# Eight places for weighted samples instead of five, and the residual's tiles in memory that is given back, in a four-layer convolution kernel

## The chip, the cores and the metric

The kernel runs on one core of a Trainium2 chip. A core has a matrix engine (TensorE, in the profile PE, its weight loads PEld), VectorE (DVE), ScalarE (ACT), GpSimd (POOL) and SyncE (SP), which here only issues DMAs. Each engine works through its own queue in order; they wait for each other through semaphores. The metric is the device time of one execution in microseconds; the time before is the median of three runs.

## The reference

Four layers follow each other on `x` of shape (2, 256, 64, 64), in float32:

```python
x = _L0_conv_ref(x, ...)   # group norm, 4-head attention over 4096 pixels, projection; xn + proj
x = _L1_conv_ref(x, ...)   # adds a position term
x = _L2_conv_ref(x, ...)   # 1x1 to 64 channels, deformable 3x3 with a mask, 1x1 back, + x, relu
x = _L3_conv_ref(x, ...)   # two deformable 3x3 convolutions with 256 channels, + x
```

The last layer is the one that the change touches. It is `h = relu(group_norm(x)); h = deform_conv(h, 1); h = relu(group_norm(h)); h = deform_conv(h, 2); return h + x`, and a deformable convolution is

```python
off = conv1x1(depthwise7x7(h)) + b          # 9 taps x (y, x) for every pixel
samp[k] = bilinear(h, base + tap[k] + off)  # four corners, weighted, for every tap k
out = einsum('bckhw,ock->bohw', samp, w)    # sum over 256 channels and 9 taps
```

So every output pixel takes 9 samples of 256 channels, each the weighted sum of four pixels at an address that the data decide.

## The kernel before

**Four layers in one program.** `attention` holds layers 0 and 1, and drips parts of layer 2 into its own steps; `deform` holds layer 3 and, beside its first steps, the second image of layer 2. The order of the instructions on TensorE, ScalarE, VectorE and GpSimd is the order in which the Python code writes them. The order of the DMAs on SP is left to a scheduler, which may put a load where its tile first has memory.

**The loop of `deform`.** Layer 3 is four passes `n`: (image 0, convolution 1), (image 1, convolution 1), (image 0, convolution 2), (image 1, convolution 2). A pass has 8 blocks (`i`) of 512 pixels, a block 9 taps (`k`), a tap 4 groups (`j`) of 128 pixels. One group of one tap is a step, so a block has 36 steps, a pass 288 and the loop 1152. A step handles 128 pixels on the 128 partitions, with all 256 channels in a row. What one turn `s` of the loop writes, in this order:

- `gather(s + 8)`: GpSimd fetches for 128 pixels the four corners, 4 x 256 values each, into one of 10 places of `four` (L848). The first 72 steps load samples that were gathered earlier, through SP (L1448).
- `left(s + 3)` and `right(s + 2)`, only for "paired" steps: ScalarE scales the left two corners (L1471), VectorE adds the right two times their share (L1477), in place. In the first pass the steps from the third block on are paired, in the other passes every second one.
- `first(s + 1)`: takes a place for `smp`, the weighted sample, and ScalarE writes the first corner times its weight into it (L1486).
- `others(s)`: VectorE adds what is left into `smp`: one instruction for a paired step (L1490), three for another (L1496).
- `evacuate`, in every fourth turn: ScalarE copies the four transposed samples of a tap from PSUM into `st` (L1517).
- `product`: TensorE multiplies a transposed sample with the weights of its tap and sums in the bank `out` of the block (L1527), two half outputs `ob` of 128 channels, one bank each.
- `turn(s - 3)`: TensorE transposes the two halves of `smp` of step s - 3 into PSUM (L1508). With this the place of that `smp` is free.
- `due`: work put off to this turn. For convolution 1 ScalarE empties a finished bank (L1552), for convolution 2 VectorE does, adding the bias and the residual (L1563); SP stores the result (L1564).
- then the side work: steps of `seconds` (the second image of layer 2, whose code is `Bottleneck.conv`), of `image` (the normalized image that the next pass samples: L1372 on ScalarE, L1382 on TensorE, L1388 on VectorE) and of `offsets` (the addresses of the next pass: L805, L825 and L839 on TensorE, L816 and L834 on ScalarE, L738 to L778 on VectorE).

**Places.** A pool with `bufs=n` gives its tiles n places in turn. A tile that takes a place waits for the last reader of the tile that had it. `smp` (pool `df_s`, L1312) has 5 places of 1 KB per partition, so the write of `smp` s + 1 waits for the transposition of s - 4. The pool `work` (L1310) has two places of each name: among them `res` (L1559), the residual of a half block, 2 KB per partition, loaded by SP at L1560 when the bank is finished, and `imgt`.

**Memory given back.** The second image of layer 2 has pools of its own in an `ExitStack` called `inner` (L1584): gathers `bfour`, sums, transposed tiles and blocks `bx`. When its last step has run, `inner.close()` (L1622) gives their memory back, and the step after that may open pools there: `image` for pass 1 opens one for `x1`, the image that L1333 loads.

Of the kernel before, what the change touches and what calls it, by code (L numbers as in the profile page):

```python
# [11 lines left out]
F32 = mybir.dt.float32  # L12
# [8 lines left out]
P = 128  # L21
# [43 lines left out]
class Net:  # L65
# [1235 lines left out]
    def deform(self, bott):  # L1301
# [4 lines left out]
        tc, nc, a = self.tc, self.nc, self.a  # L1306
        with ExitStack() as ctx:
            gp = ctx.enter_context(tc.tile_pool(name="df_g", bufs=10))
            wp = ctx.enter_context(tc.tile_pool(name="df_w", bufs=1))
            work = ctx.enter_context(tc.tile_pool(name="df_work", bufs=2))  # L1310
            cp = ctx.enter_context(tc.tile_pool(name="df_c", bufs=4))
            sp = ctx.enter_context(tc.tile_pool(name="df_s", bufs=5))  # L1312
            tp = ctx.enter_context(tc.tile_pool(name="df_t", bufs=2))
            pmisc = ctx.enter_context(tc.tile_pool(name="df_pm", bufs=1, space=PSUM))
            pdw = ctx.enter_context(tc.tile_pool(name="df_pd", bufs=1, space=PSUM))
# [11 lines left out]
            def load(b, src, pool):  # L1327
                x[b] = pool.tile([P, 2, HW], F32, name=f"x{b}")
                src = src.rearrange("(cb p) n -> p cb n", p=P)
                for i in range(4):  # L1330
                    cols = slice(1024 * i, 1024 * i + 1024)
                    queue = (nc.gpsimd, nc.sync)[b]
                    queue.dma_start(x[b][:, :, cols], src[:, :, cols])  # L1333
# [26 lines left out]
            def image(b, l):  # L1360

                if l == 0:
                    load(b, self.x2d[b], ctx.enter_context(tc.tile_pool(name="df_x1", bufs=1)))
                sc, sh = yield from self.norm_steps(
                    stats[b], bott.gmask, V_GN_G[l], V_GN_B[l], ps
                )
                yield
                v = self.img3[b].rearrange("(y x) (s c) -> y x s c", x=GW, c=C)
                for i in range(NB):
                    for cb in range(2):  # L1370
                        xs = x[b][:, cb, 512 * i : 512 * i + 512]
                        nc.scalar.activation(  # L1372
                            xs, xs, AF.Relu, scale=sc[:, cb : cb + 1], bias=sh[:, cb : cb + 1]
                        )
                        yield
                    t = work.tile([P, 4, C], F32, name="imgt")
                    for g in range(2):
                        pt = ps([P, 2, C])
                        for j in range(2):
                            px = (4 * i + g * 2 + j) * P  # L1380
                            for cb in range(2):
                                nc.tensor.transpose(  # L1382
                                    pt[:, j, cb * P : cb * P + P],
                                    x[b][:, cb, px : px + P],
                                    self.ident,
                                )
                        yield
                        nc.vector.tensor_copy(t[:, g * 2 : g * 2 + 2, :], pt)  # L1388
                        if g == 1:
                            for r in range(2):  # L1390
                                for s in range(2):
                                    y0 = 8 * i + r + 1 - s
                                    dst = v[y0 : y0 + 7 : 2, 1 : W + 1, s, :]
                                    nc.sync.dma_start(
                                        dst.rearrange("j x c -> x j c"),
                                        t[64 * r : 64 * r + 64, :, :],
                                    )
                        yield
# [39 lines left out]
            def gather(s):  # L1438
                if s < ALL:
                    n, i, k, j = parts(s)  # L1440
                    b, l = layers[n]
                    fours[s] = gp.tile([P, 4, C], F32, name="four")
                    four = fours[s].rearrange("p s c -> p (s c)")
                    if n == 0 and i < EARLY:

                        queue = nc.gpsimd if s < AHEAD else nc.sync
                        m = 4 * k + j
                        queue.dma_start(four, self.samp_d[i][m * P : m * P + P, :])  # L1448
                        return
                    idx = corners[b, l, i][0]  # L1450
                    self.gather(four, self.img3[b], idx[:, j, k : k + 1])
# [15 lines left out]
            def left(s):  # L1467

                if paired(s):
                    uv = fours[s][:, 0:2].rearrange("p s c -> p (s c)")  # L1470
                    nc.scalar.mul(uv, uv, share(s, 0, 1))  # L1471

            def right(s):
                if paired(s):
                    four = fours[s].rearrange("p s c -> p (s c)")
                    uv = four[:, : 2 * C]
                    nc.vector.scalar_tensor_tensor(  # L1477
                        uv, four[:, 2 * C :], share(s, 1, 1), uv, ALU.mult, ALU.add
                    )

            def first(s):

                if s < ALL:
                    smps[s] = sp.tile([P, C], F32, name="smp")
                    scale = share(s, 0, 0) if paired(s) else weight(s, 0)
                    nc.scalar.mul(smps[s], fours[s][:, 0], scale)  # L1486
# [27 lines left out]
            def evacuate(u):  # L1514
                if 0 <= 4 * u < ALL:
                    sts[u] = tp.tile([P, 2, 512], F32, name="st")
                    nc.scalar.copy(sts[u], pts.pop(u))  # L1517
# [23 lines left out]
            def finish(n, i, ob, s):  # L1541

                b, l = layers[n]
                out = outs[ob]
                cols = slice(512 * i, 512 * i + 512)
                rows = slice(ob * P, ob * P + P)
                bias = self.vec[:, V_CB[l] + ob : V_CB[l] + ob + 1]
                if l == 0:
                    xs = x[b][:, ob, cols]

                    def first_layer():
                        nc.scalar.activation(xs, out, AF.Identity, bias=bias)  # L1552

                    due.setdefault(s + 1, []).append(first_layer)
                    due.setdefault(s + 3, []).append(
                        lambda: nc.vector.bn_stats(stats[b][:, ob, i, :], xs)
                    )
                else:
                    res = work.tile([P, 512], F32, name="res")  # L1559
                    nc.sync.dma_start(res, self.x2d[b][rows, cols])  # L1560

                    def second_layer():
                        nc.vector.scalar_tensor_tensor(res, out, bias, res, ALU.add, ALU.add)  # L1563
                        nc.sync.dma_start(self.out[b, rows, cols], res)  # L1564

                    due.setdefault(s + 2, []).append(second_layer)
# [14 lines left out]
                            self.steps = None  # L1581

            OFFS = 24
            inner = ExitStack()  # L1584
            second = bott.conv(1, bott.pools(inner, 8, 7), ps)
            for s in range(AHEAD):
                gather(s)
# [13 lines left out]
            for s in range(ALL + 16):  # L1601
                n = s // LAYER
                if s == LAYER:
                    stats[1] = self.norm_stats()
                gather(s + AHEAD)
                left(s + 3)
                right(s + 2)
                first(s + 1)
                others(s)
                if (s - 7) % 4 == 0:  # L1610
                    evacuate((s - 7) // 4)
                product(*divmod(s - 9, 4), s)
                turn(s - 3)
                for f in due.pop(s, ()):
                    f()
                last.follow(s)
                if seconds:
                    seconds.follow(s)
                    if not seconds.steps:
                        seconds = None  # L1620
                        stats[1] = bott.stats[1]
                        inner.close()  # L1622
                        images.append(Side(s, 0.9, image(*layers[1])))
                if s % LAYER == LAYER // 2 and 1 <= n < len(layers) - 1:
                    images.append(
                        Side(s, IMAGE / (LAYER // 2 - LEAD - 12), image(*layers[n + 1]))
                    )
                if s % LAYER == LAYER - LEAD - 8 and n + 1 < len(layers):
                    for o in images + offs:
                        for _ in o.steps or ():  # L1630
                            pass
                    images, offs = [], []
                    offs.append(Side(s, OFFS / BLOCK, offsets(*layers[n + 1])))
                for o in images + offs:
                    o.follow(s)
# [101 lines left out]
```

## Time and profile before

| | |
|---|---|
| median of 3 runs | 5122.12 us (5121.92 to 5128.18) |
| profiled execution | 5119.31 us |
| its span, first to last instruction | 5117.5 us |
| mean granted TensorE clock | 0.972 of full speed |
| busy: PE, DVE, ACT, POOL | 94%, 79%, 64%, 45% of the span |
| `deform` loop | 2990 us to the end |
| ACT writes of `smp` (L1486) | 1152, about 0.5 us each |
| transpositions (L1508) | 2304, 0.27 us each as modelled |

How to read it: the profile is one execution, its times are counted from the start of the span. A line of a wait list names the instruction that waited, then what released it. Matmul ends are modelled, and matmuls overlap, so a busy TensorE is not TensorE at its peak, and two transpositions that follow each other start closer together than one takes. "issue" as a releaser means that the engine waited for nothing that the profile shows. A name as L1486 is a line of the kernel before.

### The profile page before, as it was taken

Reading aid. Unit: us, or ns where it says so; the run is one execution under the profiler, and the core shown is the slowest. Engines: PE = TensorE matmul, PEld = TensorE weight load, DVE = VectorE, ACT = ScalarE, POOL = GpSimd, SP = SyncE. Lnnn points to the kernel's source line nnn. Section 1 sums busy time; section 2 is a strip of 40 time slices with the busy share of each in tenths; the row PEclk is TensorE's granted clock in tenths of the full one; section 3 lists DMA queues with packets and bytes.
Section 4 is the critical chain, followed back from the end, with each engine's and each line's share of the span. In section 5 each row is a group of like instructions: output and inputs, shape, how many; then the busy total and the mean of one; then the engine's idle time right before and its main releaser. Section 6 shows DMA issues by size and latency. Waiting matters only on the chain. (4 is left out here: it accounts for less than half of the span.)

```text
span 5117.5 us, 100364 instructions
## 1 busy us (share of the span) xinstructions
PE 4793.9 (94%) x38200; PEld 2669.1 (52%) x38200; DVE 4025.2 (79%) x7281; ACT 3251.1 (64%) x5869; POOL 2325.6 (45%) x2256
## 2 busy tenths in 40 slices
PE   8999999999999999999999956678999999999998
PEld 5555565555565555565555523334444444444444
DVE  6878867878768888677767668867788888888888
ACT  5676656666666666666656622247876766666666
POOL 0111111111106777565123257775777666666665
PEclk9999999999999999999999977779999999999999
DMA  5231121111112333332547767679999999999998
GB/s 173 61 97 53 43 69 49 35 47 31 55 53 80 103 98 105 93 86 70 164 147 284 274 223 236 202 237 349 358 339 352 363 376 358 366 396 344 349 352 331
DMA packets 367025, 997.68 MB, mean 195 GB/s; under 512 B 61372, under 2 KB 98810, under 8 KB 366542
## 3 DMA queue, kind: packets, MB, share of 16 engines
q0 software_dynamic: 196560, 690.41, 37.4%
q1 hardware_dynamic: 169438, 300.73, 18.0%
q8 instruction: 300, 4.92, 0.4%
q14 instruction: 183, 1.50, 0.1%
q10 hardware_dynamic: 544, 0.13, 0.0%
HBM read 855.36 MB, written 127.35 MB: 192 GB/s over the span
## 5 line engine op out<-in xcount | busy, mean ns | idle before, releaser
L598 ACT ACTIVATE e<-sc,low 128x1024 f32<-128x1024 f32 x1024 | 1146.2, 1119 | 742.3 <-DVE low L592 738.0
L848 POOL DMA_INDIRECT four<-img,didx x1080 | 1152.6, 1067 | 549.9 <-issue 140.3
L592 DVE TENSOR_REDUCE low<-sc 128x1 f32<-128x1024 f32 x1024 | 1205.0, 1218 | 231.7 <-PE sc L580 227.3
L1527 PE MATMUL out<-st,wc 128*128 128x512 f32 x2304 | 1224.8, 614 | 85.7 <-ACT st L1517 41.5
L580 PE MATMUL sc<-k,qs 64*128 64x512 f32 x2048 | 999.1, 606 | 0.5 <-DVE k L368 0.3
L639 PE MATMUL av<-et,v 128*64 128x256 f32 x8192 | 997.7, 386 | 0.0
L580 PE MATMUL sc<-k,q 64*128 64x512 f32 x2048 | 978.2, 605 | 0.0
L519 POOL TENSOR_TENSOR o<-o,f 128x1024 f32<-128x1024 f32 x63 | 149.5, 2373 | 1765.2 <-DMA f<-share_d 1007.7
L610 PEld LDWEIGHTS tt<-ident,e 64*128 64x128 f32 x16384 | 655.3, 139 | 512.9 <-issue 272.7
L629 ACT COPY et<-tt 128x512 f32<-128x512 f32 x1152 | 658.4, 584 | 171.8 <-PE tt L610 170.8
L610 PE MATMUL tt<-ident,e 64*128 64x64 f32 x16384 | 728.0, 227 | 36.3 <-ACT et L629 17.7
L627 DVE COPY et<-tt 128x512 f32<-128x512 f32 x896 | 612.5, 684 | 161.5 <-PE tt L610 160.9
L1496 DVE SCALAR_TENSOR_TENSOR smp<-four,dw,smp 128x256 f32<-128x256 f32 x1296 | 627.2, 484 | 140.5 <-ACT smp L1486 109.0
L639 PEld LDWEIGHTS av<-et,v 128*64 128x64 f32 x8192 | 554.0, 137 | 300.9 <-issue 48.4
L848 POOL DMA_INDIRECT bfour<-img,bidx x576 | 584.1, 1014 | 183.9 <-issue 94.8
L1508 PEld LDWEIGHTS pt<-ident,smp 128*128 128x128 f32 x2304 | 330.5, 144 | 633.9 <-issue 470.9
L1471 ACT ACTIVATE four<-four,dwt 128x512 f32<-128x512 f32 x648 | 465.0, 718 | 200.1 <-DMA four<-img,didx 196.6
L1477 DVE SCALAR_TENSOR_TENSOR four<-four,dwt 128x512 f32<-128x512 f32 x648 | 484.9, 748 | 112.6 <-ACT four L1471 110.2
L1527 PEld LDWEIGHTS out<-st,wc 128*128 128x128 f32 x2304 | 390.9, 196 | 339.3 <-issue 222.8
L580 PEld LDWEIGHTS sc<-k,qs 64*128 64x128 f32 x2048 | 346.9, 189 | 208.7 <-issue 116.8
L1508 PE MATMUL pt<-ident,smp 128*128 128x128 f32 x2304 | 448.8, 278 | 4.6 <-DVE smp L1496 3.1
L805 PE MATMUL pd<-x,wf 128*126 128x512 f32 x840 | 436.0, 601 | 0.0
(189 smaller groups left out, 4743.1 us busy)
## 6 DMA issues: line engine op xcount, KB each, us to landing
f<-share_d SPq DMA_DIRECT2D x128, 256.0 KB
four<-samp_d SPq DMA_DIRECT2D x64, 512.0 KB
xb<-xn SPq DMA_DIRECT2D x55, 512.0 KB
img<-imgt SPq DMA_DIRECT2D x96, 256.0 KB
four<-img,didx POOLq DMA_INDIRECT x1080
xa<-res SPq DMA_DIRECT2D x32, 512.0 KB
samp_d<-xb SPq DMA_DIRECT2D x32, 512.0 KB
xb<-in_x SPq DMA_DIRECT2D x20, 512.0 KB
```

What stands on the lines that cost most here:

```text
L580: nc.tensor.matmul(s[:, j, :], lhsT=q[u, i // 2][int(h != j)][halves[j], at : at + P], rhs=k[u][c][halves[j], h, :], start=True, stop=True,)
L592: nc.vector.tensor_reduce(low, s, AX.X, ALU.max, negate=True)
L598: nc.scalar.activation(e.rearrange("p j n -> p (j n)"), s, AF.Exp, bias=blk.low[:, g, c : c + 1], accum_out=blk.sum[:, g, c : c + 1],)
L610: nc.tensor.transpose(pt[:, m, :], e[half, m // 4, m % 4 * P : m % 4 * P + P], self.ident[half, half],)
L627: nc.vector.tensor_copy(dst, pt)
L629: nc.scalar.copy(dst, pt)
L639: nc.tensor.matmul(now["av"][halves[h], :], lhsT=v[u][c][:, m, halves[h]], rhs=ets[j][:, m, h, :], start=(m == 0), stop=(m == 7),)
L848: self.nc.gpsimd.indirect_dma_start(out=dst, out_offset=None, in_=img, in_offset=bass.IndirectOffsetOnAxis(ap=idx, axis=0),)
L1477: nc.vector.scalar_tensor_tensor(uv, four[:, 2 * C :], share(s, 1, 1), uv, ALU.mult, ALU.add)
L1496: nc.vector.scalar_tensor_tensor(smps[s], four[:, c], weight(s, c), smps[s], ALU.mult, ALU.add)
L1508: nc.tensor.transpose(pts[u][:, c, j * P : (j + 1) * P], smp[:, c * P : c * P + P], self.ident,)
L1527: nc.tensor.matmul(outs[ob], lhsT=wc[k][:, c, ob * P : ob * P + P], rhs=sts[u][:, c, :], start=(k == 0 and c == 0), stop=(k == K2 - 1 and ...
```

## The change

Three edits in `deform`. The pool of `smp` gets eight places of 1 KB instead of five, 3 KB per partition more. The two places of `res`, 4 KB per partition, leave the pool `work` and get a pool of their own, `df_r`, which is opened right after `inner.close()`, so in memory that the second image of layer 2 gave back. What is computed stays the same, and so do the instructions of the five engines.

```diff
@@ deform
-            sp = ctx.enter_context(tc.tile_pool(name="df_s", bufs=5))
+            sp = ctx.enter_context(tc.tile_pool(name="df_s", bufs=8))
@@ deform, finish
-                    res = work.tile([P, 512], F32, name="res")
+                    res = places["res"].tile([P, 512], F32, name="res")
                     nc.sync.dma_start(res, self.x2d[b][rows, cols])
@@ deform
-            inner = ExitStack()
+            inner, places = ExitStack(), {}
             second = bott.conv(1, bott.pools(inner, 8, 7), ps)
@@ deform, in the loop
                         inner.close()
+                        places["res"] = ctx.enter_context(tc.tile_pool(name="df_r", bufs=2))
                         images.append(Side(s, 0.9, image(*layers[1])))
```

## The prediction

> **What bounds the kernel now.** I read the busy times first, then a table of the deform part by stretches, then the waits of ScalarE and TensorE there, then one stretch in order of time.
>
> ```profile
> PE 4793.9 (94%) x38200; PEld 2669.1 (52%) x38200; DVE 4025.2 (79%) x7281; ACT 3251.1 (64%) x5869; POOL 2325.6 (45%) x2256
> ```
>
> TensorE is busy 94% of the span. The change touches only the deform loop, which starts at 2990 us (the first transposition of `smp`). Busy times there, by stretch (time, PE, PEld, DVE, ACT, POOL, granted clock, DMA share, GB/s):
>
> ```profile
> 2990.00:3513.00 523.00, 346.16 (x1090) 163.15 (x1089) 414.75 (x946) 183.83 (x322) 383.81 (x371) 0.77 0.73 240
> 3513.00:3979.00 466.00, 451.92 (x1658) 224.12 (x1657) 381.07 (x814) 363.17 (x636) 327.37 (x295) 0.99 0.96 357
> 3979.00:4275.00 296.00, 286.60 (x1066) 143.67 (x1065) 262.20 (x582) 207.86 (x363) 198.20 (x187) 0.99 0.98 367
> 4275.00:4560.00 285.00, 277.46 (x1033) 139.19 (x1032) 253.45 (x566) 197.31 (x341) 189.23 (x179) 1.00 0.99 372
> 4560.00:4603.00 43.00, 42.43 (x149) 21.68 (x148) 37.85 (x86) 29.07 (x51) 28.76 (x28) 1.00 1.02 396
> 4603.00:5002.00 399.00, 377.58 (x1355) 185.29 (x1354) 339.28 (x747) 262.18 (x454) 260.19 (x251) 1.00 0.96 350
> 5002.00:5117.00 115.00, 95.51 (x345) 46.54 (x343) 96.74 (x205) 74.72 (x131) 67.61 (x65) 1.00 0.86 328
> ```
>
> Up to 3513 GpSimd sets the pace: 371 instructions, busy 383.8 us, with about 0.30 us between two gathers (the releaser "issue", 0.3 us at most in the first 330 us) make 383.8 + 371 x 0.30 = 495 of 523 us. From 3513 to 5002 TensorE does: 95 to 99% busy at a granted clock of 0.99 to 1.00. So ScalarE's waits count only so far as they reach TensorE. ScalarE's two largest waits from 3513 on (total, times, longest):
>
> ```profile
> ACT smp L1486 <- PE pt L1508: 282.0, 330, 2.6
> ACT four L1471 <- DMA four<-img,didx: 115.6, 116, 3.8
> ```
>
> The 282.0 us are what the change aims at: a write of a new `smp` that waits for the transposition of an old one. Beside them, what TensorE itself waited for in the same stretch:
>
> ```profile
> PE out L1527 <- ACT st L1517: 18.0, 19, 3.1
> PE out L1527 <- DVE res L1563: 16.7, 16, 2.1
> PE out L1527 <- DVE floor L756: 14.0, 8, 1.8
> PE pm L1382 <- ACT x L1372: 11.5, 7, 4.7
> PE pm L1382 <- DVE imgt L1388: 5.3, 5, 2.0
> ```
>
> With four small groups (1.7, 1.0, 0.4, 0.2) that is 68.8 us: the most that a quicker ScalarE or VectorE can return from 3513 on. The "floor" group is the bank of a finished block too: L756 follows L1563 in VectorE's order.
>
> **The change part by part.** No instruction is added, removed or reordered on TensorE, VectorE, ScalarE or GpSimd; only waits differ, and two DMAs move on SP.
>
> *Eight places.* Before, L1486 at step s writes `smp` s+1 over that of s-4, transposed in step s-1. After, it is that of s-7, transposed in step s-4: three steps of slack more. But every fourth step ScalarE's L1517 copies four finished transpositions out, and waits for the last, made in the step before: the very bound that five places set. The lead is given back at each L1517; three steps in four run free. What that is worth shows near the end of a block (start, duration, instruction, idle before):
>
> ```profile
> 4607.66 0.51 ACT L1486 ACTIVATE smp<-four,dw 128x256 f32<-128x256 f32 x1 [1.81 <-PE pt L1508]
> ...
> 4608.20 1.52 DVE L1496 SCALAR_TENSOR_TENSOR smp<-four,dw,smp 128x256 f32<-128x256 f32 x3 [1.51 <-ACT smp L1486]
> ...
> 4610.23 0.99 ACT L1517 COPY st<-pt 128x1024 f32<-128x1024 f32 x1
> ...
> 4617.98 0.75 DVE L1563 SCALAR_TENSOR_TENSOR res<-out,vec,res 128x512 f32<-128x512 f32 x1
> ...
> 4618.87 1.10 PE L1527 MATMUL out<-st,wc 128*128 128x512 f32 x2 [1.72 <-DVE floor L756]
> ```
>
> From 4608.2 VectorE runs without a gap until TensorE has waited twice (1.72 us here, 1.31 us at 4622.58). With eight places the first line starts 1.81 us earlier and the second 1.51. But L1517 must still wait for the transposition that starts at 4609.40 and takes 0.38: it moves from 4610.23 to 4609.8, and the L1471 behind it from 4611.13 to 4610.75. VectorE's next L1477 (4612.28) reads what that leaves 0.7 us later, so starts at 4611.55. Its lead has shrunk from 1.5 to 0.72 us; from there it is continuous, L1563 and the product come 0.72 earlier, and the second wait keeps its length. So 0.72 us a block, of 3.03 waited. By stretch:
>
> - 4603 to 5002: seven such blocks, 7 x 0.72 = 5.0 of 21.4 us waited (bounds 0 and 21.4; the worked block decides).
> - 4275 to 4603: L1563 six times, 3.4 us. At 4328.83 ScalarE waits 2.65 us and again only L1517's 0.43 stays: 6 x 0.43 = 2.6. The waits for L1372 and L1388 (4.6) have a write held 0.83 us ahead of an L1372 that comes 1.21 late; half, 2.3. Together 4.9 (0 to 8.0).
> - 3979 to 4275: 9.4 us waited: L1388 and L1372 5.0, half is 2.5; L1496, L1517 and L834 4.0 in eight waits, a 0.2 each is 1.5. Together 4.0 (0 to 9.4).
> - 3513 to 3979: 14.0 us, of which 4.7 is L1372 behind the load of `x1` and stays; 6.5 is L1517, late because L1471 waits 34.6 us for gathers, which no place for `smp` brings sooner. I take 2.0 (0 to 9.3).
> - 5002 to 5117: 16.1 us; ScalarE waits 20.6 us for gathers, only 6.7 for transpositions. One block as above and a little: 1.0 (0 to 16.1).
> - 2990 to 3513: ScalarE waits 24.7 + 1.1 us for transpositions up to 3500, GpSimd's issue covers it: 0 (0 to 25.8).
>
> Sum: 16.9 us.
>
> *Waits that change engine.* In the built program ScalarE loses 598 semaphore instructions (L1486 869 fewer, L1517 274 more), and VectorE gains 432, nearly all before L1490, which now names the transposition that its ScalarE write no longer implies. They ask for a `smp` eight steps back, long transposed, so nothing queues behind them. Such an instruction on VectorE's queue (least, median, most ns):
>
> ```profile
> L1496 DVEq EVENT_SEMAPHORE  x506: 21/21/50, 2986.3 to 5102.9; - x169
> ```
>
> L1490 to L1496, with one between, start 0.39 us apart at 4610.31 (0.48 long); L1477 to L1490, with none, 0.67 (0.75 long): the overlap is 0.08 either way. I take 0; the bounds are 0 and 432 x 0.021 = 9.1 us, or 21.6 at the longest.
>
> *The residual's tiles.* The first two loads of L1560, at 2971.44, go behind the last L1078 of the second layer (3484.09) and ahead of its last store L1169 (3501.70) on SP. Issue is 0.82 us for both; 512 KB at 357 GB/s are 1.5 us, and 17 us are free: 0. Were they late, that store, the load of `x1` and the L1372 that already waits 6.2 us would slip by up to 1.5. At 2971 SP next issues at 2981.87, so what they leave gains nothing, 1.5 at most. Their first use is at 4276. GpSimd's queue is not passed.
>
> **Sum.** The profiled execution took 5119.3 us (span 5117.5), the median of the runs is 5122.1, 2.8 more. 5119.3 - 16.9 = 5102.4, and with 2.8 more 5105.
>
> **The rivals.** A measurement of this kernel can tell about 0.2% (10.2 us) from no change: 5111.9 to 5132.4.
>
> *Transfers hold it.* From 3513 to 4603 the DMA share is 0.96 to 1.02, and ScalarE waits 115.6 us for gathers in all. If they can come no faster, only the last two stretches gain: 6.0 us, 5116. Against it: 396 GB/s from 4560 to 4603, where others ran at 357 to 372. The Trainium skill, DMA: Bandwidth & Descriptors, Specifications, gives about 358 GB/s of HBM per core; by it the stretches at 357 to 372 have nothing left and 5116 is the time. The trace differs: it shows 396.
>
> *All bubbles go.* If the lead adds up over steps, TensorE's waits without the 4.7 for `x1` vanish: 64.1 us, 5058. For it: VectorE still idles 109.0 us for L1486 after 3513. Against it: L1517 every fourth step. The Trainium skill, Perfetto Trace Analysis, Identifying Performance Opportunities, says that the same gap repeating can mean too few buffers; by it this would be the case. The trace agrees on the repeating gap, and puts L1563 and L1517 at its end, not `smp`.
>
> *Slower: VectorE pays for the moved waits.* It is 85% busy from 4603 to 5002 and unbroken where TensorE waits. At 50 ns each and no gain, 432 cost 21.6 us: 5144. It decides from 24 ns each on (10.2 / 432) if nothing is gained, from 63 ns with 16.9 gained. Against it: the equal overlap above.
>
> **How the numbers follow.** Forecast (10 to 30 us gained) 0.52; transfers hold it, or the lead is given back entirely, 0.27; all bubbles (30 to 64) 0.11; slower 0.10. Faster 0.52 + 0.11 = 0.63, same 0.27, slower 0.10. The range runs from 5086, which leaves out most of the bubbles' case, to 5124, which leaves out the slower one; the forecast alone is 5092 to 5112.
>
> **What would show it.** L1486 waiting for L1508 falls from 282 to under 80 us, and L1517, which waited 3.7, takes over some 100 or more. TensorE's waits for L756 and L1563 between 4603 and 5002 fall from 3.03 to about 2.3 a block; the stretch up to 3513 keeps its length. The forecast is wrong if TensorE's waits stay at 68.8 us, if L1471's wait for gathers grows by what L1486's loses and TensorE's follow, or if VectorE's busy runs grow longer for the same instructions.

## The result and the profile after

The changed kernel takes 5109.08 us (median of 9 runs, 5106.65 to 5112.29), the kernel before in the same comparison 5123.53 us (9 runs, 5120.43 to 5130.29). The ratio is 0.9971, with a 95% interval of 0.9960 to 0.9981: 14.5 us faster, 4.1 us above the forecast of 5105. The profiled execution takes 5109.1 us, its span 5107.3 us.

Busy times of the changed kernel on its page, and then by stretch of the deform loop (time, PE, PEld, DVE, ACT, POOL, granted clock, DMA share, GB/s):

```profile
PE 4791.3 (94%) x38200; PEld 2668.7 (52%) x38200; DVE 4014.1 (79%) x7281; ACT 3234.4 (63%) x5869; POOL 2324.2 (46%) x2256
```

```profile
3513.00:3979.00 466.00, 454.15 (x1664) 226.92 (x1663) 382.72 (x832) 362.87 (x641) 326.79 (x296) 1.00 0.96 360
3979.00:4275.00 296.00, 289.69 (x1092) 145.10 (x1091) 263.94 (x591) 209.74 (x369) 202.16 (x191) 1.00 0.99 375
4275.00:4603.00 328.00, 320.32 (x1198) 161.38 (x1196) 291.00 (x654) 224.43 (x395) 218.30 (x208) 1.00 0.99 377
4603.00:5002.00 399.00, 382.77 (x1376) 187.63 (x1373) 339.24 (x757) 257.86 (x459) 265.90 (x255) 1.00 0.97 354
5002.00:5117.00 115.00, 89.95 (x307) 44.21 (x306) 88.79 (x188) 68.00 (x119) 61.85 (x59) 0.96 0.78 304
```

The instruction counts of the page are those of before. TensorE fills 382.77 instead of 377.58 us of the stretch from 4603 to 5002, with 1376 matmuls instead of 1355: the same kind of work, packed closer. From 4275 to 4603, 320.32 us stand against 277.46 + 42.43 = 319.89. Busy time shows nearly nothing there, though 1198 matmuls stand against 1033 + 149 = 1182; the table below shows a gain. Now the waits of ScalarE from 3513 on (total, times, longest):

```profile
ACT st L1517 <- PE pt L1508: 201.6, 146, 3.3
ACT four L1471 <- DMA four<-img,didx: 163.6, 147, 3.6
ACT smp L1486 <- DVE four L1477: 72.1, 79, 2.0
```

The 282.0 us that L1486 waited for a transposition are gone without a rest. But ScalarE waits as long as it did: its three largest groups and L1517's 3.7 were 282.0 + 115.6 + 46.9 + 3.7 = 448.2 us, and the three lines above with two small groups (L834 7.2, L816 4.8) are 449.3. The wait has moved to the copy L1517 and to the gathers. VectorE's waits do the same. It waited 109.0 us at L1496 for L1486, and 64.6 at L1477 for L1471:

```profile
DVE four L1477 <- ACT four L1471: 164.5, 158, 5.7
...
DVE smp L1496 <- ACT smp L1486: 3.0, 8, 0.6
```

106.0 us go in the one place and 99.9 come in the other. What counts is TensorE:

```profile
PE out L1527 <- ACT st L1517: 13.4, 13, 2.6
PE out L1527 <- DVE res L1563: 13.3, 14, 1.3
PE out L1527 <- DVE floor L756: 8.1, 8, 1.1
PE pm L1382 <- ACT x L1372: 6.5, 7, 1.4
PE pm L1382 <- DVE imgt L1388: 5.0, 5, 1.9
```

With the smaller groups these are 53.1 us instead of 68.8, 15.7 less. From 4617 to 5017 lie seven blocks of one kind, the last of the third pass and six of the fourth; they are called the blocks of the fourth pass below. The end of one of them, in order of time, shows the step that the prediction worked out:

```profile
4668.74 1.01 ACT L1517 COPY st<-pt 128x1024 f32<-128x1024 f32 x1 [1.37 <-PE pt L1508]
...
4670.98 0.75 DVE L1563 SCALAR_TENSOR_TENSOR res<-out,vec,res 128x512 f32<-128x512 f32 x1
...
4671.87 1.10 PE L1527 MATMUL out<-st,wc 128*128 128x512 f32 x2 [1.06 <-DVE floor L756]
...
4673.06 0.51 ACT L1486 ACTIVATE smp<-four,dwt 128x256 f32<-128x256 f32 x1 [1.27 <-DVE four L1477]
...
4675.57 0.70 PE L1527 MATMUL out<-st,wc 128*128 128x512 f32 x1 [1.31 <-DVE res L1563]
```

TensorE's two waits are 1.06 (0.99 to 1.06 in these blocks) and 1.31 us, where they were 1.72 and 1.31. L1486 now waits for VectorE, not for TensorE, and L1517, which comes every fourth step, waits for the transposition.

Where the time went, taken between the same instructions of TensorE in both traces and counted from the loop's first transposition (a step is a turn of the loop, and its transposition a pair of L1508):

| from | to | before us | after us | change | forecast |
|---|---|---|---|---|---|
| first L1508 | first L1382 (3518) | 525.65 | 526.79 | +1.1 | 0 |
| first L1382 | second group norm's L152 (3979) | 460.85 | 458.03 | -2.8 | -2.0 |
| that L152 | transposition of step 617 (4275.72, after 4274.79) | 296.41 | 290.82 | -5.6 | -4.0 |
| step 617 | step 833 (4616.77, after 4613.82), six blocks | 341.05 | 339.03 | -2.0 | -4.9 |
| step 833 | step 1085 (5017.09, after 5008.95), seven blocks | 400.32 | 395.13 | -5.2 | -5.0 |
| step 1085 | end of the span | 100.45 | 98.36 | -2.1 | -1.0 |
| sum | | 2124.73 | 2108.16 | -16.6 | -16.9 |

The changed kernel's loop begins 6.3 us later (2999.15 against 2992.81), after code that is the same in both. In the other executions on chips that run the kernel before in 5122 us, the first transposition lies at 2990.4 to 2999.2, the first row varies from -5.2 to +1.9 us and the second from -3.1 to +3.2, with no clear relation to the number of places: neither these rows nor the later begin are put down to the change. From the second group norm on, the rows add up to -14.9 us here, which is what was forecast for them, and to -13.7, -14.8, -12.7 and -12.7 in the runs below with eight, nine, seven and six places.

### The profile page after: what moved, and what is told of

Read it like the earlier page. It is cut to its first block, busy times and chain, and to the rows that moved or that the text cites. A ratio compares the mean times of both kernels' runs of the same rounds, so it can differ in the third digit from the quotient of the medians.

```text
span 5107.3 us, 100192 instructions
## 1 busy us (share of the span) xinstructions
PE 4791.3 (94%) x38200; PEld 2668.7 (52%) x38200; DVE 4014.1 (79%) x7281; ACT 3234.4 (63%) x5869; POOL 2324.2 (46%) x2256
## 5 line engine op out<-in xcount | busy, mean ns | idle before, releaser
L1508 PEld LDWEIGHTS pt<-ident,smp 128*128 128x128 f32 x2304 | 331.2, 144 | 637.5 <-issue 491.3
L1496 DVE SCALAR_TENSOR_TENSOR smp<-four,dw,smp 128x256 f32<-128x256 f32 x1296 | 626.4, 483 | 34.8 <-ACT smp L1486 3.0
L1477 DVE SCALAR_TENSOR_TENSOR four<-four,dwt 128x512 f32<-128x512 f32 x648 | 485.3, 749 | 213.4 <-ACT four L1471 211.3
L1471 ACT ACTIVATE four<-four,dwt 128x512 f32<-128x512 f32 x648 | 466.2, 719 | 249.4 <-DMA four<-img,didx 245.1
L1508 PE MATMUL pt<-ident,smp 128*128 128x128 f32 x2304 | 448.6, 277 | 5.6 <-DVE smp L1490 3.6
```

Of the source, the lines that this page charges most:

```text
L1496: nc.vector.scalar_tensor_tensor(smps[s], four[:, c], weight(s, c), smps[s], ALU.mult, ALU.add)
L1508: nc.tensor.transpose(pts[u][:, c, j * P : (j + 1) * P], smp[:, c * P : c * P + P], self.ident,)
```

## The experiments

Theory: the extra places free three steps in four; the copy L1517, which waits for the last of four transpositions every fourth step, gives the lead back, and near a block's end VectorE's unbroken run decides. Rivals: the gathers' transfers hold ScalarE; each place adds its share; the move of the residual's tiles does something of its own. The first four kernels ran on one chip with the kernel before (5122.53 us, 5119.42 to 5128.7, 23 runs).

**The residual's tiles alone.** Five places, the rest of the change as it is:

```diff
-                    res = work.tile([P, 512], F32, name="res")
+                    res = places["res"].tile([P, 512], F32, name="res")
...
-            inner = ExitStack()
+            inner, places = ExitStack(), {}
...
                         inner.close()
+                        places["res"] = ctx.enter_context(tc.tile_pool(name="df_r", bufs=2))
```

> Five places for smp as before, the residual's tiles in the memory given back. Theory 1 (the gain is the slack of the smp places, three steps in four; the residual's move is neutral): within 5 us of the kernel before, L1486 waits for L1508 about 280 us after 3513 as before. Rival (the move itself makes the gain, by an emptier pool or a quieter SP queue at 2971): 10 us or more below before.

Measured: 5121.7 us (5117.4 to 5132.7), ratio 1.0001 (0.9992 to 1.0010). L1486 waits 276.6 us for L1508, TensorE 18.6 for L1517, 14.7 for L1563 and 14.0 for L756: the kernel before. From the second group norm on its rows differ from those before by -0.5, +0.1, 0.0 and -0.9 us, which is how far two executions of equal work lie apart there. No cost or gain of the move can be seen; the change is the places.

**Eight places again**, the changed kernel on the same chip as the others.

> The changed kernel again, beside the others on one chip. All theories: about 14 us below before (5108 to 5111).

Measured: 5104.96 us (5098.61 to 5108.19), ratio 0.9968 (0.9955 to 0.9980). The rows of the table come again from the second to the last: 1.6, 4.4, 2.0, 5.2 and 2.0 us less.

**A ninth place.**

```diff
-            sp = ctx.enter_context(tc.tile_pool(name="df_s", bufs=8))
+            sp = ctx.enter_context(tc.tile_pool(name="df_s", bufs=9))
```

> Nine places, residual moved. Theory 1 (L1517 gives the lead back every fourth step, so a ninth place frees nothing): within 3 us of eight places, and TensorE's first wait per block from 4603 to 5002 stays at 0.99 to 1.06 us. Rival (the lead adds up over steps with every place): another 3 to 5 us below eight.

Measured: 5105.19 us (5102.72 to 5106.82), ratio 0.9965 (0.9953 to 0.9977). ScalarE's waits with nine places, 3513 to 5117:

```profile
ACT st L1517 <- PE pt L1508: 214.3, 151, 3.3
ACT four L1471 <- DMA four<-img,didx: 151.6, 147, 3.3
```

Equal to eight: once L1486 waits for no place, another place frees nothing.

**The copy and its products one step later**, with eight places. If L1517 alone gave the lead back, it would now be kept longer.

```diff
-                if (s - 7) % 4 == 0:
-                    evacuate((s - 7) // 4)
-                product(*divmod(s - 9, 4), s)
+                if (s - 8) % 4 == 0:
+                    evacuate((s - 8) // 4)
+                product(*divmod(s - 10, 4), s)
```

> Eight places, and L1517 with the products behind it one step later in the loop, so that ScalarE may be two steps behind the transposition it copies instead of one. Theory 1 (L1517 is the cap): TensorE's two waits per block from 4603 to 5002 fall from 2.30 us to about 1.2, the L1563 waits from 4275 on from 0.43 to under 0.2; 6 to 10 us below eight places, with 1 us of it lost to the longer tail. Rival (the gathers are the cap): within 2 us of eight places, and ScalarE's wait for gathers (L1471) takes over what L1517 no longer waits.

Measured: 5110.81 us (5107.25 to 5115.83), ratio 0.9977 (0.9968 to 0.9986): 6 us above eight, where a gain of 6 to 10 was expected; the two intervals overlap. ScalarE's waits, 3513 to 5117, and then TensorE's from 4603 to 5002:

```profile
ACT four L1471 <- DMA four<-img,didx: 219.3, 208, 5.3
ACT smp L1486 <- DVE four L1477: 99.5, 102, 3.9
ACT st L1517 <- PE pt L1508: 51.1, 64, 3.3
ACT od L834 <- PE pd L825: 41.6, 24, 2.7
```

```profile
PE out L1527 <- DVE res L1563: 13.9, 14, 1.1
```

In the fourth pass it does what the theory says, but little of it: L1517's wait falls from 201.6 to 51.1 us, TensorE's two waits from 16.2 to 13.9 us in seven blocks, and the block from 56.62 to 56.25 us. ScalarE's lead goes to the gathers, to VectorE and to L834 instead. What is lost in this execution is lost elsewhere: 1.9 us more than the kernel before up to the first L1382, 3.0 more from there to the second group norm, 2.1 less from there to step 617, where eight places take 4.4 to 5.6 less, and 0.8 more in the tail instead of 2.0 to 2.1 less. Why the later copy costs there was not tried; it stays open. So L1517 is a cap, but not the only one.

**Half the gathers' bytes.** If transfers held the loop, moving half as much would free it. Three kernels, with five places, with eight, and with eight and the later copy; a fourth, with the whole gathers, five places and the residual's tiles moved, gives the gathers an eleventh place. In the first three the two right corners are left out and the two left ones taken in their stead, so their output is another one. The edit of the first three, and of the last:

```diff
-                    self.gather(four, self.img3[b], idx[:, j, k : k + 1])
+                    self.gather(four[:, : 2 * C], self.img3[b], idx[:, j, k : k + 1])
...
-                        uv, four[:, 2 * C :], share(s, 1, 1), uv, ALU.mult, ALU.add
+                        uv, uv, share(s, 1, 1), uv, ALU.mult, ALU.add
...
-                            smps[s], four[:, c], weight(s, c), smps[s], ALU.mult, ALU.add
+                            smps[s], four[:, c % 2], weight(s, c), smps[s], ALU.mult, ALU.add
```

```diff
-            gp = ctx.enter_context(tc.tile_pool(name="df_g", bufs=10))
+            gp = ctx.enter_context(tc.tile_pool(name="df_g", bufs=11))
```

> The kernel before, but each gather of layer 3 fetches only the two left corners (2 KB instead of 4 KB per pixel) and the two right ones are taken from them: less data to move, the same instructions otherwise. Both theories: ScalarE's wait for gathers (L1471) after 3513 falls from 116 us to under 20; its L1486 waits for L1508 stay at 250 us or more. As a kernel it is 5 to 40 us below before, from the stretches where gathers are late; TensorE's two waits per block from 4603 to 5002 stay at 3.0 us.

> The changed kernel with the same halved gathers. Theory 1 (L1517 alone gives the lead back): eight against five places is worth 12 to 18 us here too, the two waits per block stay at about 2.3 us, and the L1563 waits from 4275 on at 0.43. Rival (late gathers eat the rest of the lead): more than 20 us below the halved kernel with five places, the waits from 4275 on under 0.2.

> Halved gathers, eight places, and L1517 with the products one step later. If late gathers are what kept the later copy from gaining: 6 to 10 us below halved eight, two waits per block at 1.3 us or less. If VectorE or the od and wide copies hold it: within 3 us of halved eight or above it.

> The memory that the residual's move frees is given to the gathers instead: five places for smp as before, eleven for four instead of ten. Theory 1 (smp's places hold ScalarE): within 5 us of before, L1486 still waits 270 us or more for L1508. Rival (any deeper buffer helps): 10 us or more below before, ScalarE's wait for gathers halved.

These four ran on another chip, on which the kernel before takes 5292.23 us (5272.78 to 5305.71, 31 runs), so their times stand only beside that one. The blocks of the fourth pass are taken from a transposition to the one 36 steps later:

| kernel | us | ratio | 95% interval | median of seven blocks, us | their sum, us |
|---|---|---|---|---|---|
| half, five places | 5290.38 | 0.9997 | 0.9982 to 1.0013 | 57.35 | 400.2 |
| half, eight places | 5301.97 | 1.0026 | 1.0009 to 1.0043 | 56.80 | 399.0 |
| half, eight, later copy | 5279.82 | 0.9975 | 0.9960 to 0.9990 | 56.25 | 395.2 |
| whole, eleven gather places, five samples | 5301.52 | 1.0019 | 1.0005 to 1.0032 | 57.35 | 400.8 |

Most of the expectations for whole times missed: half the bytes with five places gain 1.9 us instead of 5 to 40, and eight places then lose 11.6 instead of gaining 12 to 18. The loop of the half kernel with five places is later here: its first L1382 comes at 3637.4, and its seven blocks lie from 4793 to 5193. The granted clock is 0.74 up to that L1382, 0.98, 0.97 and 0.99 in the next three rows of the table, and only in the seven blocks is it 1.00 as on the other chips. There the blocks can be compared. The seven blocks before, then with half the bytes and five places, and two of ScalarE's waits of that kernel from 3513 on:

```profile
4618.00:5018.00 400.00, 378.91 (x1358) 185.84 (x1358) 340.53 (x750) 262.69 (x455) 259.49 (x252) 1.00 0.96 348
```

```profile
4794.00:5194.00 400.00, 378.91 (x1358) 185.70 (x1358) 340.24 (x750) 262.06 (x455) 262.12 (x252) 1.00 0.65 184
```

```profile
ACT smp L1486 <- PE pt L1508: 354.8, 309, 5.5
...
ACT four L1471 <- DMA four<-img,didx: 19.8, 13, 3.2
```

184 GB/s instead of 348, and the wait for gathers is down from 115.6 to 19.8 us, yet the seven blocks take 400.2 us, as before with whole gathers (400.3). With five places transfers hold nothing there. Two blocks of the third pass that ran at clock 1.00 say the same: 61.47 and 60.21 us with half the bytes against 61.44 and 60.17 before, and with eight places 61.12 and 59.84 against 61.11 and 59.83 in the changed kernel. For the other stretches this chip decides nothing.

With eight places and half the bytes, three of the seven blocks take the 56.6 to 56.7 us of the changed kernel; the others are 0.3 to 1.5 us longer than there, and their sum is only 1.2 us below five places instead of 5.2. It is not the gathers: ScalarE waits for none of them in these blocks, but 19.7 us in all where the profile names no releaser ("issue") or one outside the traced instructions ("remote"); with five places such waits are 16.2 us, and no block is longer for them. Why stays open, and with it why this kernel is slower than that with five places over the whole program. The later copy, which lost with whole gathers, is 22 us below half eight here. That is the direction that late gathers would give, but the two waits of a block are 2.3 us and not the 1.3 that were expected for that case, so this stays open too. An eleventh place for the gathers does not help: 9.3 us more than the kernel before, and L1486 still waits 292.9 us from 3513 to 5117. The changed kernel itself was not run on this chip, so nothing shows that it gains there.

**Six and seven places.** The cap by the copy and the share for each place give different curves. On a third chip, as fast as the first (the kernel before: 5122.32 us, 5114.66 to 5129.37, 14 runs), with the number in this line and the residual's tiles moved:

```diff
-            sp = ctx.enter_context(tc.tile_pool(name="df_s", bufs=5))
+            sp = ctx.enter_context(tc.tile_pool(name="df_s", bufs=6))
```

> Six places for the weighted samples, the residual's tiles made as in the changed kernel. A write of `smp` then waits for the transposition of one step earlier than with five. Theory (the lead is capped by the copy L1517 every fourth step, and by VectorE's unbroken run, not by the number of places): one step of slack, about 1.6 us, is nearly the whole 1.81 us that L1486 waited in the worked block, so six places already give two thirds or more of what eight give: ratio 0.9965 to 0.9980, 10 to 17 us below the kernel before; L1486 waits under 120 us for L1508 from 3513 on and L1517 over 60. Rival (each place adds the same share): a third, 5 us, ratio about 0.9990, L1486 still over 180 us.

> Seven places, otherwise as six. Theory of the copy as the cap: the same as eight within 3 us, ratio 0.9960 to 0.9978; L1486 waits under 60 us for L1508. Rival (each place adds the same share): two thirds of eight, 10 us, ratio 0.9980, and clearly above eight.

Measured: six 5107.91 us (5101.34 to 5111.49), ratio 0.9971 (0.9960 to 0.9982); seven 5107.09 (5104.06 to 5108.22), ratio 0.9972 (0.9961 to 0.9982). ScalarE's waits with six, 3513 to 5117:

```profile
ACT four L1471 <- DMA four<-img,didx: 158.5, 151, 3.2
ACT st L1517 <- PE pt L1508: 138.3, 149, 3.3
ACT smp L1486 <- DVE four L1477: 77.1, 76, 2.1
ACT smp L1486 <- PE pt L1508: 56.1, 89, 1.4
```

and with seven:

```profile
ACT st L1517 <- PE pt L1508: 202.8, 150, 3.3
...
ACT smp L1486 <- PE pt L1508: 1.5, 5, 0.4
```

The sixth place gives nearly all of it: the usual block of the fourth pass is 56.62 us with six, seven, eight and nine, and 57.36 with five. With six L1486 still waits 56.1 us and L1517 the rest, and their sum (194.4) is about what L1517 waits alone with seven or eight. The share for each place is out.

**VectorE relieved**, with five places and with eight. In the unpaired steps the kernel leaves the fourth corner out of the sum, so its output is another one:

```diff
-                    for c in range(1, 4):
+                    for c in range(1, 3):
```

> The kernel before with the loop of L1495 running over two corners instead of three: in the unpaired steps the fourth corner's sample is left out of the sum, so the output is another one; per block of 36 steps VectorE has 18 additions of about 0.4 to 0.5 us less, some 8 us of 49. Five places. Theory (in the fourth pass VectorE's unbroken run sets TensorE's two waits at a block's end): the waits for L756 and L1563 fall from 3.03 us a block to under 0.8, and the block from 57.36 to about 55 us. Rival (transfers or the copy L1517 set them): the block stays above 56.7 us.

> Eight places, the residual's tiles moved, and the same corner left out as in the run with five. Theory (VectorE's lead is what eight places buy): with VectorE relieved the two kernels take the same block, 55 us within 0.3, and differ by under 6 us in all (eight no more than 0.12% ahead of five) instead of 14 to 17. Rival (ScalarE's lead is worth something by itself): eight stays 10 us or more ahead of five.

Measured: five 5092.42 us (5088.17 to 5101.61), ratio 0.9950 (0.9936 to 0.9963); eight 5079.40 (5077.93 to 5081.00), ratio 0.9920 (0.9907 to 0.9934). TensorE's waits from 4603 to 5002 with five and relieved:

```profile
PE out L1527 <- DVE res L1563: 6.3, 8, 0.8
PE out L1527 <- DVE floor L756: 3.0, 7, 0.4
```

and with eight and relieved:

```profile
PE out L1527 <- DVE res L1563: 5.6, 7, 0.9
PE out L1527 <- ACT st L1517: 2.0, 1, 2.0
PE out L1527 <- DVE floor L756: 0.2, 1, 0.2
```

The block falls from 57.36 to 55.53 us with five, and from 56.62 to 55.05 with eight. VectorE's work is thus worth more to the fourth pass than the places are: relief takes 12.9 us off these seven blocks with five places, three places more take 5.2. The expectation was too strong twice. In the seven blocks (the lines above reach a little into the tail) the waits fall from 21.4 to 8.5 us with five places, and not to the 5.6 or less that was expected; L1563 still comes late, and why was not tried. And the two relieved kernels stay 13.0 us apart (10.2 by the spans of their profiled executions) where under 6 was expected: the rival that ScalarE's lead is worth something by itself holds. Between the same marks eight is ahead by 2.2 us from 3979 to step 617, by 0.7 from there to step 833 and by 2.9 in the seven blocks, about half or less of what each was without relief (5.6, 2.0 and 5.2), and by 1.5 and 2.1 before and after. From 4276 to 4617 these kernels also show what takes the images' waits over. VectorE's waits of the one with eight, 4250 to 4600:

```profile
DVE four L1477 <- ACT four L1471: 67.4, 56, 2.8
DVE imgt L1388 <- DMA img<-imgt: 8.1, 1, 8.1
```

The copy of a transposed image tile waits 8.1 us for the store of an older one, and TensorE's L1382 5.4 us for that copy.

## Why the prediction came out

*What bounds the loop, and where the lead goes back: right.* L1486's wait for L1508 went to nothing (under 80 was asked for), L1517 took 201.6 (100 or more). The prediction called L1517 the cap; nine places gain nothing over eight, and six show that a single step of slack is already nearly all that L1517 leaves. The later copy limits it: with L1517 moved back, the gathers, VectorE and L834 are next, close behind.

*0.72 us a block in the fourth pass: right.* 0.73 was measured (57.36 to 56.62, 1.72 to 0.99 at the first wait, 1.31 unchanged at the second), 5.2 us for the stretch against 5.0. It was worked from one block, instruction by instruction, and the same block after shows the steps of that working:

```profile
4606.92 1.01 ACT L1517 COPY st<-pt 128x1024 f32<-128x1024 f32 x1 [1.38 <-PE pt L1508]
...
4608.59 0.75 DVE L1477 SCALAR_TENSOR_TENSOR four<-four,dwt 128x512 f32<-128x512 f32 x1 [0.68 <-ACT four L1471]
...
4614.30 0.75 DVE L1563 SCALAR_TENSOR_TENSOR res<-out,vec,res 128x512 f32<-128x512 f32 x1
```

Counted from the transposition that L1517 waits for (4609.40 before, 4606.45 after), L1517 comes 0.36 us earlier where 0.43 was forecast, L1477 0.74 (0.73) and L1563 0.73 (0.72). That VectorE's run sets what is left is shown by the relieved kernels for the larger part.

*4275 to 4603: the step that failed.* The prediction let L1563's wait of 0.57 us shrink by L1517's 0.43 at each of six blocks, 2.6 us, and gave the images half of their 4.6, 2.3. Measured were 2.0 us in all, 0.34 in each block, in both executions of the changed kernel. TensorE's waits after, 4275 to 4603:

```profile
PE out L1527 <- DVE res L1563: 2.9, 6, 0.6
PE pm L1382 <- ACT x L1372: 2.7, 2, 1.4
PE pm L1382 <- DVE imgt L1388: 2.1, 2, 1.1
```

They were 3.4, 2.6 and 2.0. L1563 releases TensorE 0.15 us earlier in a block, not 0.43, and L1372 and L1388 come no earlier. The wait of ScalarE was the wrong thing to carry over: its lead there goes to the gathers (30.9 to 49.1 us) and to VectorE (8.1 to 14.9). The other 0.19 us of each block come from a place that the prediction did not name. The weight loads of L839 waited for ScalarE's copy L834, before, from 4276 to 4617:

```profile
PEld pd L839 <- ACT od L834: 1.2, 6, 0.3
```

After, there is no such wait. As for the images, with VectorE relieved the waits for L1372 come down to 0.6 to 0.7 us with either number of places, so there VectorE held L1372, not the places for `smp`; but those for L1388 grow to 4.8 and 5.4 us, and the images' waits together are no shorter.

*3979 to 4276: right in sign, undersized.* 5.6 us in place of 4.0 (4.4 to 5.9 in the kernels with six to nine places). The named waits of TensorE between the same marks explain 3.4 of it (9.4 to 6.0 us); the rest is left open. This term and the one before it err in opposite ways, by 1.6 and 2.9 us, so the sum was better than its parts.

*3513 to 3979 and the tail: not shown.* The first row is 2.8 and 1.6 us shorter in the two executions of the changed kernel, against a forecast of 2.0, but 0.4 to 0.7 longer with nine, seven and six places. The tail, forecast at 1.0, is 0.4 to 2.1 shorter with six to nine places and 0.9 with five and the tiles moved. That a sum of 16.9 stands beside a measured 16.6 is in part luck, since 1.7 of the 16.6 are the first two rows. The stretch before 3513 was put at 0; it varies by more than 5 us by itself, so nothing shows that either.

*The moved waits: right.* VectorE's new semaphore instructions before L1490, of which the kernel before has 11 (least, median, most ns):

```profile
L1490 DVEq EVENT_SEMAPHORE  x420: 21/21/21, 3365.4 to 5094.4; - x140
```

L1490 itself takes a median of 480 ns (479 before), and VectorE's unbroken runs end earlier, not later. The rival of a slower kernel had this price; it isn't there.

*The residual's tiles: right.* Their first loads go at 3493.7, where they were put by the prediction, L1372 waits 6.1 us where it waited 6.2, and the run with this edit alone is the kernel before.

*Transfers hold it: wrong as the whole,* though the wait for gathers grew by 48 us, which the prediction named as a sign of it. The sign counted only if TensorE's waits followed, and they fell by 15.7. The stretches that it said could not gain did: 5.6 us from 3979 to step 617, where the rate rose from 367 to 375 GB/s, and 2.0 from there to step 833. Half the bytes settle it for the fourth pass with five places. That this forecast of 5116 was no further off than 7 us shows how little a time alone can tell these cases apart. By the Trainium skill, DMA: Bandwidth & Descriptors, Specifications, about 358 GB/s of HBM per core would have left nothing to gain; the stretch from 4560 to 4603 moved 399 GB/s in the changed kernel, so the trace doesn't bear that out as a bound here.

*All bubbles go: wrong.* Of VectorE's 109.0 us of idle at L1496 106.0 did vanish, and 99.9 came back at L1477.

## What to carry to other kernels

When a wait for a buffer's place is the largest of an engine, look for the next wait in that engine's own order which asks for the same event: it caps what more places give, and a place or two beyond the old number can be all that is left to gain (here six places did nearly what eight and nine did). Work out one repeated block to the instruction that the bounding engine waits for, and do so once for every kind of block: the block worked out was right to 0.01 us, while its result carried over to blocks of another kind gave 4.9 us where 2.0 came. Add up an engine's waits over all their causes before and after; ScalarE's 448.2 us became 449.3, and only TensorE's 68.8 to 53.1 said that time was won. Take the marks between which time is compared on the engine that bounds: VectorE's first L1563 came 0.25 us after the transposition of step 617 before and 1.95 us ahead of it after, so as a mark it would put 2.2 us of VectorE's lead into the wrong row.

## What the runs showed of the chip that was not expected

One chip ran the kernel before in 5292.23 us instead of 5122.5, 3.3% longer, with granted clocks of 0.957 to 0.963 over a run where two others have 0.971 to 0.975. On it the blocks at clock 1.00 are the same: with five places and whole gathers the usual block is 57.35 us. The clock alone does not explain the rest. From the first transposition to the first L1382 that kernel takes 593.6 us instead of the 525.7 of the kernel before, at a clock of 0.75 instead of 0.78, and TensorE waits over 50 us there with no releaser in the profile, where the kernel before has no such wait. What holds it stays open. And 432 more semaphore instructions on an engine that is 85% busy, at 21 ns each, cost it nothing that could be measured.
